# A planned order with the first scan step ranked ahead, and 360 filler products in place of 480

## The chip, the cores and the metric

The kernel runs on one core of one Trainium2 chip. The metric is device time in microseconds of one execution; before the change the median of three runs was 3912.99 us (3912.96 to 3919.06).

## What is computed

A block of four sublayers on an input of 8 batches x 512 tokens x 256 channels, in float32. Each sublayer is added to its input, which goes through a layer norm first:

```python
x = x + attention(layernorm(x), ...)
x = x + fp4_ffn(layernorm(x), w_gate, w_up, w_down)
x = x + mamba(layernorm(x), ...)
x = x + fp4_ffn(layernorm(x), w_gate, w_up, w_down)
```

- The attention has 16 heads of 16 channels, brought to 32 latent channels, with rotary positions, a causal mask and a softmax.
- The FFN has 704 hidden channels. Input, hidden and weights are quantised in blocks of 16 to a four-bit grid and scaled back; the gate goes through a SiLU.
- The mamba sublayer has a second norm and a residual of its own, a projection to 2 x 512 channels, and for each of two directions (forward, and backward in time) a causal convolution of 4 taps, a SiLU, and the recurrence `h = exp(dt*A)*h + dt*B*u`, `y = sum over 16 states of h*C`. The two results are merged by a product, gated and projected back.

## The kernel before

**The work of one batch.** All 512 tokens of a batch are handled together, channels on the 128 partitions and time along the row, or tokens on the partitions where a norm needs it. There are five kinds of work, each written as a Python generator that yields after every small piece:

- `attention`: projections into latents, `heads` for four groups of four heads (maxima of the scores by `L658`, `L660`, `L663`, `L668`; scores again, exponentials and products with the values by `L689`, `L691`, `L694`, `L699`), and the result x1 (`L584`, `L585`).
- `ffns`: `ffn_front` (norm by `L496`, quantising by `L723` to `L735`), `ffn_hidden` (`L802` to `L804`), `ffn_down` (`L818` to `L829`), in four blocks of 128 tokens. The first FFN reads x1 and stores x2; the second reads x4 and stores the output.
- `mamba_pre`: norm, projection, and eight convolutions (`L923` loads a diagonal filter, `L927` multiplies, `L928` to `L930` make the SiLU), whose results go to DRAM.
- `ssm_prep`: the products that give dt, B and C (`dbt` by `L1022`, dt by `L1038` to `L1052`), four times a batch.
- `ssm`, the scan, and `merge`, which makes x4.

**The scan** has 512 steps: 8 batches x 2 directions x 4 blocks of 128 channels x 8 pairs of states. One step multiplies `ub` by a row of B that is replicated over the partitions (`L1081`, DVE), computes two exponentials (`L1084`, ACT), scans twice (`L1086` forward or `L1088` backward, DVE), multiplies by a replicated row of C (`L1095`, POOL) and adds eight PE transposes into the PSUM tile `y` (`L1098`). The tile `h` has four buffers (`NHB`), `y` has one bank. Each step loads two replicas of 512 KB (`rep`).

**The order.** `interleave` runs the generators side by side: while batch b is scanned, batch b+3's attention, batch b+1's `mamba_pre`, batch b+2's first FFN and batch b-1's merge and second FFN are issued. For batch 0 there is a prologue without a scan: attention of batches 0 and 1, the first FFN and `mamba_pre` of batch 0. Then `issue_in_order` (L138) throws away the order of writing. It collects all instructions with their dependences and the buffer turns of each tile (`rings`), gives each a cost, and computes a rank from the end backwards: own cost plus the largest rank among those that need it or wait for its buffer. Then it plays the program through with these costs. An engine that is free takes, of what is ready, the instruction with the highest rank. The order that results is fixed by dependences, engine by engine. It is an order, not a timing: on the chip each engine works off its queue, and waits at its head by semaphores.

**The fillers.** In the prologue, `FILL` products of two constant tiles are written into a tile of the `y` bank (`L1189`). Nobody reads them. The order gives them rank -1, below everything, and each an earliest time in the planner's clock, 70000 ns plus 600 ns per filler: PE takes one whenever nothing else is ready. Since they hold the only `y` bank, the first transposes of the scan come after the last filler.

```python
idle = psum("y")
for _ in range(FILL):
    PE.matmul(idle.rearrange("p (a k) -> p a k", a=NT), idb, idb[:, None, :].to_broadcast([P, NT, P]), start=True, stop=True)
```

Of the kernel before, what the change touches and what calls it, by code (L numbers as in the profile page):

```python
# [59 lines left out]


DMA_LAT = 2300


def accesses(i):
# [72 lines left out]
def issue_in_order(tc, traced, rings, idle):  # L138
# [8 lines left out]
    hist, users, writers = {}, {}, {}  # L147
    for k, i in enumerate(ops):
        for name, lo, hi, p0, p1, _, psum, wr in acc[k]:
            h = hist.setdefault(name, [])  # L150
# [45 lines left out]
    port = [shared_port(i, a) for i, a in zip(ops, acc)]  # L196
    dma = [type(i).__name__ == "InstDMACopy" for i in ops]
    rank = [0.0] * n
    for k in reversed(range(n)):
        rank[k] = costs[k][1] * (1.2 if ops[k].engine == mybir.EngineType.DVE else 1.0) + DMA_LAT * dma[k] + max([rank[j] for j in succ[k] + behind[k]], default=0.0)  # L200
    at = [0.0] * n
    for c, k in enumerate(users[idle[0]]):
        rank[k], at[k] = -1.0, idle[1] + idle[2] * float(c)
# [9 lines left out]
    for _ in range(n):  # L213
        best = None
        for e, q in later.items():
            r, t = ready.setdefault(e, []), free.get(e, 0.0)
            while q and q[0][0] <= t:
                k = heapq.heappop(q)[1]
# [7 lines left out]
        while q and q[0][0] <= t:  # L226
            k = heapq.heappop(q)[1]
            heapq.heappush(r, (-rank[k], k))
        k = heapq.heappop(r)[1]
# [3 lines left out]
        if dma[k]:  # L233
            t = max(t, flying[0])
            m = ways(ops[k])
            lines[:m] = [max(t + 800, x) + costs[k][1] for x in lines[:m]]
            end = max(lines[:m]) + DMA_LAT - 800
            heapq.heapreplace(flying, end)
# [32 lines left out]
def tile_hybrid(ctx: ExitStack, tc: tile.TileContext, w: dict, consts: bass.AP, out: bass.AP):  # L271
# [18 lines left out]
    rings = {}  # L290
# [875 lines left out]
    def thread_s(b):  # L1166
        for d in range(2):
            nxt = None
            for k, _ in enumerate(ssm(b, d, scrs[b])):
                if k % 16 == PREP_AT:  # L1170
                    nxt = next(todo, None)
                    nxt = nxt and nxt()
                if nxt is not None and k % PREP_EV == 0:
                    next(nxt, None)
                yield
                if nxt is not None and k % 16 == 15:
                    for _ in nxt:
                        pass

    NA_, NB_, NS_ = 80, 100, 80  # L1180
    FILL, FILL_FROM, FILL_GAP = 480, 70000, 600
    PREP_AT, PREP_EV = 2, 2
    prep = {}
    af = {}
# [21 lines left out]
    first = thread_s(0)  # L1206
# [3 lines left out]
    for b in range(1, B):  # L1210
        run((NS_, OS, thread_s(b)), (NA_, OA, thread_a(b + 3)), (NB_, OB, thread_b(b - 1, b + 1, b + 2)))
    run((NB_, OB, thread_b(B - 1, B, B)))
    issue_in_order(tc, nc.cur_bb.bb.instructions, rings, (idle.name, FILL_FROM, FILL_GAP))


# [30 lines left out]
```

## Time and profile before

| | us |
|---|---|
| median of three runs | 3912.99 |
| the profiled execution | 3908.11 |
| its span (first to last instruction) | 3906.3 |
| PE busy | 3215.2 (82%) |
| DVE busy | 2953.2 (76%) |
| POOL busy | 2111.9 (54%) |
| ACT busy | 1740.7 (45%) |
| fillers (L1189): 480 records of 379 ns | first at 90.5, last at 641.5 |
| scan, first and last start on DVE (L1081) | 553.6 and 3772.0 |
| scan, first and last transposes on PE (L1098) | 642.0 and 3779.6 |

All times within the execution are counted from the first instruction. Records of PE products overlap, since the next one enters while the last one drains, so their sum is more than the time that PE is taken for. PEclk is the share of full clock that PE was granted. "Stretch" views give busy time of each engine between two moments; "by source line" views give, for one line of the kernel, its instructions with shortest, median and longest duration in ns and the first and last start in us.

### The profile page before, as it was taken

The page shows a single profiled execution, that of the slowest core. Times are in us where ns is not written, and L with a number is a line of the kernel's source. Part 1 is how long each engine was busy: PE and PEld are TensorE (multiplying, and loading weights), DVE is VectorE, ACT ScalarE, POOL GpSimd, SP SyncE. Part 2 cuts the span into 40 slices and gives each one's busy share as a digit, 9 for nine tenths or more (in the row PEclk, how much of TensorE's full clock was granted, in tenths as well). Part 3 has the DMA queues.
Part 4 walks back from the last instruction along what each step waited for, and adds up shares of the span by engine and source line. Part 5 has one row for each costly group of instructions (what it writes and reads, how often), then busy time and mean ns, then how long its engine had stood idle before and what let it go on. Part 6 is the DMA issues. An engine that isn't in the chain of part 4 may idle for free. (4 is left out here: it accounts for less than half of the span.)

```text
span 3906.3 us, 43657 instructions
## 1 busy us (share of the span) xinstructions
PE 3215.2 (82%) x13444; PEld 1843.7 (47%) x13444; DVE 2953.2 (76%) x3803; ACT 1740.7 (45%) x2989; POOL 2111.9 (54%) x1714
## 2 busy tenths in 40 slices
PE   5999999798889888798778888798878767767676
PEld 3444444444444545455444554445444544444553
DVE  5325256878988689886987779887888988888873
ACT  2222343555465344453455444554455445543421
POOL 4103134665675466654775546655576676666642
PEclk7999999899989988899889998799888978978888
DMA  6222354888777977689667896779767886995942
GB/s 167 82 80 69 121 192 131 269 282 271 232 263 257 304 241 238 212 274 294 218 222 231 258 297 204 245 254 315 236 218 261 290 314 215 326 352 174 366 151 71
DMA packets 439799, 898.19 MB, mean 230 GB/s; under 512 B 65005, under 2 KB 220046, under 8 KB 439566
## 3 DMA queue, kind: packets, MB, share of 16 engines
q1 hardware_dynamic: 439566, 895.40, 69.3%
q8 instruction: 108, 1.77, 0.2%
q14 instruction: 125, 1.02, 0.1%
HBM read 783.61 MB, written 103.15 MB: 227 GB/s over the span
## 5 line engine op out<-in xcount | busy, mean ns | idle before, releaser
L1095 POOL TENSOR_TENSOR h<-h,rep 128x1024 f32<-128x1024 f32 x512 | 1217.1, 2383 | 856.5 <-DVE h L1088 303.9
L1084 ACT ACTIVATE a<-dt,Aneg 128x512 f32<-128x512 f32 x1024 | 697.7, 689 | 561.4 <-DVE h L1088 265.1
L1098 PE MATMUL y<-cst,h 128*128 128x128 f32 x4096 | 693.5, 298 | 180.2 <-POOL h L1095 179.6
L1081 DVE TENSOR_TENSOR h<-ub,rep 128x1024 f32<-128x1024 f32 x512 | 616.6, 1210 | 206.7 <-PE y L1098 95.2
L1098 PEld LDWEIGHTS y<-cst,h 128*128 128x128 f32 x4096 | 529.7, 153 | 412.9 <-POOL h L1095 236.3
L1086 DVE TENSOR_TENSOR_SCAN h<-a,h 128x512 f32<-128x512 f32 x512 | 601.3, 1206 | 52.4 <-ACT a L1084 46.6
L1088 DVE TENSOR_TENSOR_SCAN h<-a,h 128x512 f32<-128x512 f32 x512 | 600.1, 1208 | 48.1 <-ACT a L1084 40.9
L314 PE MATMUL pb<-wgu,fxT 128*128 128x512 f32 (+1 forms) x768 | 372.9, 596 | 23.0 <-DVE hff L804 14.1
L699 PE MATMUL pa<-pt,vs 128*32 128x128 f32 (+3 forms) x1024 | 371.1, 458 | 13.0 <-ACT pt L694 10.3
L314 PE MATMUL pb<-qv,hff 128*128 128x256 f32 x1024 | 303.0, 422 | 85.3 <-DMA qv<-sy 74.6
L694 ACT ACTIVATE pt<-pa 128x512 f32<-128x512 f32 x320 | 190.3, 595 | 350.0 <-PE pa L691 347.8
L927 PE MATMUL pb<-xs,tmpB 128*128 128x512 f32 x512 | 272.6, 652 | 41.1 <-DMA tmpB<-dg_d 31.1
L658 PE MATMUL pa<-kst,qst 96*128 96x512 f32 (+3 forms) x512 | 211.2, 456 | 60.3 <-DVE mx L668 32.7
L314 PEld LDWEIGHTS pb<-qv,hff 128*128 128x128 f32 x1024 | 194.9, 209 | 137.9 <-issue 57.0
L314 PE MATMUL pb<-wdn,hT 128*128 128x256 f32 (+1 forms) x768 | 228.4, 420 | 18.1 <-ACT hT L821 7.1
L689 PE MATMUL pa<-qst,kst 98*128 98x512 f32 (+3 forms) x512 | 227.5, 449 | 14.3 <-ACT pt L694 12.2
L668 DVE TENSOR_REDUCE mx<-pa 128x1 f32<-128x512 f32 (+2 forms) x384 | 179.9, 501 | 61.4 <-PE pa L660 60.9
L314 PEld LDWEIGHTS pb<-wgu,fxT 128*128 128x128 f32 x768 | 134.3, 199 | 126.2 <-issue 85.5
L689 PEld LDWEIGHTS pa<-qst,kst 98*128 98x128 f32 x512 | 100.7, 197 | 180.8 <-issue 106.3
L314 PEld LDWEIGHTS pb<-wdn,hT 128*128 128x128 f32 (+1 forms) x768 | 142.5, 206 | 72.2 <-issue 28.4
L658 PEld LDWEIGHTS pa<-kst,qst 96*128 96x128 f32 x512 | 105.8, 209 | 133.7 <-DVE mx L668 43.1
L927 PEld LDWEIGHTS pb<-xs,tmpB 128*128 128x128 f32 x512 | 95.5, 208 | 132.7 <-issue 83.9
(217 smaller groups left out, 4882.3 us busy)
## 6 DMA issues: line engine op xcount, KB each, us to landing
rep<-bcd SPq DMA_DIRECT2D x1024, 512.0 KB
hld<-hl SPq DMA_DIRECT2D x64, 512.0 KB
hff<-in_merge_w SPq DMA_DIRECT2D x128, 256.0 KB
qv<-sy SPq DMA_DIRECT2D x128, 256.0 KB
kst<-hld SPq DMA_DIRECT2D x192, 128.0 KB
qst<-hld SPq DMA_DIRECT2D x192, 128.0 KB
tmpB<-dg_d SPq DMA_DIRECT2D x64, 256.0 KB
sxc<-tmpB SPq DMA_DIRECT2D x64, 256.0 KB
```

The source lines that it names most:

```text
L314: PE.matmul(o, L, R, start=start, stop=stop, **kw)
L658: PE.matmul(o[:, at : at + n], qst[pr][:96, j, i * P : (i + 1) * P], kst[:96, j, :n], start=(k == 0), stop=False)
L689: PE.matmul(o[:, at : at + n], kst[:, j, kt * P : (kt + 1) * P], qst[pr][:, j, kt * P :], start=(k == 0), stop=False)
L694: S.activation(pt, o, AF.Exp)
L699: PE.matmul(po[c : c + 32, kt * P :], vs[:, kt, h * VW : h * VW + 32], pt[:, at : at + n], start=(kt == 0), stop=(kt == 2), tile_position= ...
L927: PE.matmul(o, dg[:, k, :], xs[:, at : at + T], start=(k == 0), stop=(k == 3))
L1081: V.tensor_tensor(h, ub[:, None, :].to_broadcast([P, 2, T]), rb, ALU.mult)
L1084: S.activation(a, dt[:, m % 2, :], AF.Exp, scale=Aneg[:, d, m, 2 * n + e : 2 * n + e + 1])
L1086: V.tensor_tensor_scan(h[:, e], a, h[:, e], 0.0, ALU.mult, ALU.add)
L1088: V.tensor_tensor_scan(h[:, e, ::-1], a[:, ::-1], h[:, e, ::-1], 0.0, ALU.mult, ALU.add)
L1095: G.tensor_tensor(h, h, rc, ALU.mult)
L1098: PE.matmul(y[:, i * P : (i + 1) * P], h[:, e, i * P : (i + 1) * P], ident, start=(n == 0 and e == 0 and i == 0), stop=(n == NS // 2 - 1 a ...
```

## The change

The rank of one instruction, the first `L1081` of the scan, is raised by a million. Ranks are computed backwards, so every instruction that this step needs, directly or through others, or through a buffer that must come free, has a rank over a million too, and is taken before all that the first step does not need. Nothing after the first step changes its rank. The number of fillers goes from 480 to 360; their earliest times stay, 600 ns apart from 70000, so it is the last 120 that are gone. Four lines are added, and later lines stand 4 lower in the changed kernel (L1098 is L1102 there).

```diff
 DMA_LAT = 2300
+FIRST = 1e6
...
     rank = [0.0] * n
+    first = min(users[name][0] for name in rings["h"][1])
     for k in reversed(range(n)):
         rank[k] = costs[k][1] * (1.2 if ops[k].engine == mybir.EngineType.DVE else 1.0) + DMA_LAT * dma[k] + max([rank[j] for j in succ[k] + behind[k]], default=0.0)
+        if k == first:
+            rank[k] += FIRST
...
-    FILL, FILL_FROM, FILL_GAP = 480, 70000, 600
+    FILL, FILL_FROM, FILL_GAP = 360, 70000, 600
```

## The prediction

> **What bounds the kernel now.** I read the slices of the page first, to see where each engine is full.
>
> ```profile
> PE   5999999798889888798778888798878767767676
> ...
> DVE  5325256878988689886987779887888988888873
> ...
> PEclk7999999899989988899889998799888978978888
> ```
>
> A slice is 97.7 us. In slices 2 to 7 PE is full and DVE is at two to five tenths; from the seventh or eighth on DVE is near nine and PE near eight. So the kernel is two regimes: a PE-bound beginning without scan, and then the scan of 512 steps with DVE the fuller engine. Next I asked for busy times by stage (stretch, length, then busy us of PE, PEld, DVE, ACT, POOL, then clock, DMA share, GB/s):
>
> ```profile
> 289.00:406.00 117.00, 114.42 (x460) 52.48 (x458) 58.57 (x122) 32.29 (x69) 34.61 (x49) 1.00 0.22 70
> 406.00:553.00 147.00, 142.21 (x512) 60.96 (x512) 44.82 (x99) 61.70 (x107) 33.40 (x70) 0.99 0.47 148
> 553.00:642.00 89.00, 87.13 (x334) 38.34 (x332) 58.71 (x101) 32.07 (x62) 31.16 (x26) 1.00 0.41 128
> 642.00:1185.00 543.00, 458.14 (x1964) 254.08 (x1964) 464.10 (x580) 299.09 (x500) 343.15 (x271) 0.92 0.79 261
> 1200.00:2900.00 1700.00, 1432.71 (x6140) 835.63 (x6140) 1402.55 (x1753) 817.79 (x1389) 992.48 (x757) 0.91 0.76 249
> ```
>
> DVE works 58.57 of 117, 44.82 of 147 and 58.71 of 89 us, and then 85% in the fourth stretch. What separates the regimes is the line of the filler products, and the two lines of the scan beside it, in the answers by source line (L1189; then L1081 and L1098, both between 540 and 700 us):
>
> ```profile
> L1189 PE MATMUL y<-idb x480: 376/379/609, 90.5 to 641.5; 128*128 128x512 bf16 x160
> ```
>
> ```profile
> L1081 DVE TENSOR_TENSOR h<-ub,rep x14: 1186/1216/1225, 553.6 to 695.7; 128x1024 f32<-128x1024 f32 x14
> ```
>
> ```profile
> L1098 PE MATMUL y<-cst,h x89: 272/273/422, 642.0 to 699.8; 128*128 128x128 f32 x89
> ```
>
> The first scan step starts on DVE at 553.6. Its transposes into y start at 642.0, just after the last filler at 641.5: fillers own the only y bank. With four h buffers, four steps run and then the scan stands still until 646.8 (start of the fifth). That is a hole of 65 us in the scan, in a stretch where DVE has room.
>
> **What the change moves.** I compared the two built orders, fillers left out. They are the same up to the instruction that starts at 288 us on DVE and 294 us on PE, and the same again from 1166 (ACT) to 1208 us (SP) until the end: 2666 of 3805 DVE instructions and 7216 of PE's 10172 lie in the equal end. From about step 96 of the scan, then, the program is the old one, shifted. Only the shift is to be found. What lies after it, about 2700 us and the final merge and FFN, I cost at nothing, since it issues the same instructions in the same order.
>
> **Part 1, 120 fillers fewer.** Fillers follow each other in 0.216 us (starts of neighbouring records; the 379 ns of the row overlap). 120 x 0.216 = 25.9 us of PE time. Up to the split the old order has 332 fillers and the new one 337, so 148 are left in the old and 23 in the new. By itself that is worth between 0 and 26 us, as far as PE is the bound; it also frees the y bank early. The cover for fillers that stay is the wait of the attention chain before 289 us, where nothing changes.
>
> **Part 2, the first step earlier.** Its chain is attention of batch 0 (done in the equal part), FFN, mamba_pre, ssm_prep. Rows (L735 and L829 in the FFN of batch 0, and the same two lines in the last FFN, which runs alone):
>
> ```profile
> L735 POOL TENSOR_TENSOR fxn<-qv,qns x2: 1056/1056/1056, 306.7 to 310.8; 128x512 f32<-128x512 f32 x2
> ...
> L829 SPq DMA_DIRECT2D sx<-xrf x4: 342/343/425, 367.3 to 406.7; - x4
> ```
>
> ```profile
> L735 POOL TENSOR_TENSOR fxn<-qv,qns x2: 1056/1056/1056, 3854.7 to 3858.9; 128x512 f32<-128x512 f32 x2
> ...
> L829 SPq DMA_DIRECT2D out<-xrf x4: 332/338/338, 3886.2 to 3903.7; - x4
> ```
>
> From quantised input to last store: 406.7 - 310.8 = 95.9 us early, 3903.7 - 3858.9 = 44.8 us alone. In the new order a few attention products of batch 1 still stand between, so I take 51: stored at 362. Then 30.1 us to the first convolution, as before (406.7 to 436.8): 392.
>
> ```profile
> L927 PE MATMUL pb<-xs,tmpB x64: 591/593/697, 436.8 to 537.8; 128*128 128x512 f32 x64
> ```
>
> Eight convolutions start there at 436.8 to 521.1, 12.0 us apart. In the new order PE has 40 us of work between the first and the last start; the closest pairs anywhere in the trace stand 7.2 to 8.0 us apart. 7 x 8 = 56: last start at 448. Then 9.7 us to dbt (521.1 to 530.8) and 22.8 to the first h (530.8 to 553.6): **480 us instead of 553.6**. Bounds: 458 if all steps go as when alone, 508 if the FFN gains half as much and the convolutions stay 10 us apart. What the chain issues besides are loads on SP's queue: two replicas of 512 KB a step. The DMA share is 0.22 to 0.47 before 642, against 0.79 after, so there is room. POOL is 30% (34.61 of 117) and 23% busy there, room again.
>
> **Part 3, what is now behind.** Work that was ahead of the scan is behind it. I summed the orders with one cost for each form of instruction from this trace (DVE: median duration; PE: start to next start where PE is back to back, so 0.91 us for a 128x512 f32 product, 0.11 for a transpose, 0.216 for a filler). Ahead of the first y stand 554 us of PE work before, 365 after; ahead of step 24, 643 and 465; ahead of step 45, 740 and 672; ahead of step 96, 981 and 955. On DVE, ahead of the same steps: 227 and 175; 391 and 295; 497 and 476; 782 and 782. So 189 us of PE work leave the way of the scan, and 163 of them come back before step 96, most between steps 24 and 45. The sum is then made in three stretches, with DVE at the rate it held after the hole (step 4 to 96: 492 us of work in 646.8 to 1185.8, 0.913) and PE at 0.95, its rate between 289 and 642, and the larger of the two counts:
> - steps 0 to 24: DVE 121 / 0.913 = 132 us; PE 100 / 0.95 = 105. Takes 132.
> - steps 24 to 45: DVE 181 / 0.913 = 198; PE 207 / 0.95 = 218. PE ends last: 218.
> - steps 45 to 96: DVE 305 / 0.913 = 334; PE 283 / 0.95 = 298. Takes 334.
>
> 480 + 132 + 218 + 334 = 1164, where before step 96 started at 1185.8: **22 us earlier**. A gain of 74 us at the first step, and a hole of 65 us closed, shrinks since the two engines then have little slack left. The wait that takes the hole's place is DVE's and the scan's for PE in the second stretch. Bounds for this part: with DVE at 0.95 throughout, 127 + 218 + 321 = 666; with DVE at the 0.845 of the later batches (64 steps from 160 on: 367 us of DVE work in 436 us), 143 + 218 + 361 = 722. I take 0.913, as the nearest stretch with the same kind of work.
>
> The row that speaks against fewer fillers: where PE is kept full the granted clock is 1.00 (289 to 406), and in 642 to 1185, with PE 84% busy, 0.92. The new order leaves about 135 us of PE work in the 190 us before the first y, so the clock there should fall. [...]
>
> **Rivals.**
> A, DVE stays full all the way and the PE pile hides beside it: 607 us of DVE work / 0.95 = 639, 480 + 639 = 1119, 67 us earlier: **3846**. For it: 1135 to 1250 runs with both engines over nine tenths. Against: 207 us of PE work in 21 steps cannot go faster than 207.
> B, slower: the work of batches 1 and 2 that was put behind meets the scan between steps 24 and 45, and DVE and PE wait for each other as in the later batches (rate 0.845): 480 + 722 = 1202, 16 us later: **3929**. It decides from a stretch 24 to 45 over 240 us, or a DVE rate under 0.885 throughout. For it: new demand on both engines (PE 590, DVE 607 us of work) is nearer to the later batches' proportion than to that of 642 to 1185. Against: in the old order PE had to finish the same work, and did it while DVE idled.
> C, the change gives nothing: the first step's chain is not PE-bound but a chain of waits, the first h comes at 500 to 510, and the 22 us are gone: **3913**.
>
> **How the numbers follow.** The profiled execution took 3908.1 us (span 3906.3 and 1.8 around it); 3908.1 - 22 = 3886. The median of the three runs is 3913.0, 4.9 above that execution, so I forecast 3913 - 22 = **3891**. Chances: the forecast, 8 to 45 us gained, 0.48; A, more than that, 0.14; C, within 8 us (0.2%, about what a measurement of this kernel tells from no change), 0.15; B 0.23. So faster 0.62, same 0.15, slower 0.23. Range: from the best bounds (first h at 458, rate 0.95: 458 + 666 = 1124, 62 us gained) to B with a little to spare: 3850 to 3932.
>
> **What would show it.** First h at 480 (458 to 508), first y within 10 us of it, with no filler between; no pause of 65 us after the fourth step. Step 24 at about 612, step 45 at 830, step 96 at 1164, and all later steps earlier by the same amount. PE over 93% busy between steps 24 and 45. A first h after 510, or a step 45 after 850, would make the prediction wrong on the slow side; a step 45 before 800 on the fast side. If later steps are not shifted alike, the equal order did not carry the shift.

## The result

The changed kernel is slower, by 0.4%. Median of ten runs 3928.8 us (3920.93 to 3939.03) against 3912.97 us (3903.37 to 3921.88): ratio 1.0039, 95% interval 1.0027 to 1.0051. Forecast were 3891 us, in a range from 3850 to 3932, and faster with a chance of 0.62. The time lies in the range, the direction is wrong. It is the time of rival B (3929), though not for all of B's terms, as is shown further down.

The slices of the page after:

```profile
PE   5998888998979888798768888798887767767676
...
DVE  5324478668789779886987779887888988889873
...
PEclk7999989999989988899889998899888878978988
```

Slices are counted from 0 here (the prediction counts from 1). In 5 and 6 (491 to 687 us) DVE is at seven and eight tenths, where it was at five and six: the scan is early. But PE is at eight in slices 3 to 6 and no longer full, and in 7 and 8, where PE is at nine, DVE falls back to six. The same by stretches (length; busy us of PE, PEld, DVE, ACT, POOL; clock; DMA share; GB/s), first the changed kernel:

```profile
289.00:456.00 167.00, 148.15 (x475) 66.13 (x473) 57.21 (x113) 58.22 (x107) 43.55 (x66) 0.95 0.31 104
456.00:640.00 184.00, 146.21 (x622) 79.16 (x622) 148.33 (x187) 92.95 (x153) 108.19 (x84) 0.88 0.74 241
640.00:745.00 105.00, 102.02 (x419) 49.44 (x418) 64.95 (x110) 33.50 (x70) 32.83 (x27) 1.00 0.43 132
745.00:850.00 105.00, 93.79 (x377) 48.83 (x376) 70.91 (x109) 58.06 (x99) 55.30 (x61) 0.97 0.74 236
850.00:1200.00 350.00, 301.18 (x1253) 160.44 (x1252) 289.00 (x376) 181.12 (x310) 201.92 (x172) 0.92 0.73 236
1200.00:2900.00 1700.00, 1432.28 (x6140) 832.09 (x6139) 1400.37 (x1753) 808.58 (x1371) 989.72 (x759) 0.91 0.77 249
```

and the kernel before, cut at the same moments:

```profile
289.00:456.00 167.00, 163.02 (x657) 73.10 (x655) 75.20 (x164) 51.05 (x104) 45.67 (x88) 1.00 0.28 88
456.00:640.00 184.00, 178.79 (x641) 78.07 (x639) 86.89 (x157) 74.69 (x132) 53.50 (x57) 0.99 0.46 145
640.00:745.00 105.00, 87.49 (x412) 51.29 (x412) 80.20 (x104) 53.28 (x93) 57.08 (x44) 0.92 0.80 251
745.00:850.00 105.00, 85.33 (x373) 46.14 (x371) 86.76 (x105) 62.98 (x98) 69.48 (x47) 0.89 0.84 273
```

From 456 to 640 DVE does 148 us of work in place of 87, and PE 146 us in place of 179. From 640 to 850 it is the other way round: PE is 93% busy, and DVE has only 136 of 210 us, where it had 167. The last stretch, 1200 to 2900, is within 3 us of what it was (the row of the kernel before is in the prediction).

Now the lines that answer to those of before, by source line. Fillers, first scan product on DVE, transposes into y:

```profile
L1193 PE MATMUL y<-idb x360: 376/379/496, 89.6 to 302.5; 128*128 128x512 bf16 x180
```

```profile
L1085 DVE TENSOR_TENSOR h<-ub,rep x512: 1149/1211/1226, 456.3 to 3795.2; 128x1024 f32<-128x1024 f32 x171
```

```profile
L1102 PE MATMUL y<-cst,h x4096: 270/273/477, 462.7 to 3802.8; 128*128 128x128 f32 x196
```

The change did what it says: the last filler is at 302.5 in place of 641.5, the first step at 456.3 in place of 553.6, the first y 6.4 us behind it. What it gave up is in the line that ends a group of four heads (`L711`, L715 after), for batch 1, before and after:

```profile
L711 DVE TENSOR_TENSOR ya<-pa,rd x4: 425/425/425, 330.2 to 476.0; 128x256 f32<-128x256 f32 x4
```

```profile
L715 DVE TENSOR_TENSOR ya<-pa,rd x4: 424/424/425, 369.5 to 572.6; 128x256 f32<-128x256 f32 x4
```

The last group of batch 1 ends 97 us later. So the scan's first step comes 97 us earlier, and the end of that attention 97 us later. Along the scan, the lead of the changed kernel (starts of L1081 and L1085) is 97.3 us at step 0, 157.0 at step 24, 32.5 at step 45, 0.1 at step 70, and a lag of 15.8 at step 96. From there the lag stays between 11 and 19 us up to step 390; at the last step it is 23.2, and at the end 20.1 (spans of 3926.4 and 3906.3).

### The profile page after: what moved, and what is told of

Read it like the earlier page. It is cut to its first block, busy times and chain, and to the rows that moved or that the text cites. A ratio compares the mean times of both kernels' runs of the same rounds, so it can differ in the third digit from the quotient of the medians.

```text
span 3926.4 us, 43406 instructions
## 1 busy us (share of the span) xinstructions
PE 3202.5 (82%) x13324; PEld 1838.5 (47%) x13324; DVE 2964.7 (76%) x3803; ACT 1740.8 (44%) x2989; POOL 2114.5 (54%) x1714
## 5 line engine op out<-in xcount | busy, mean ns | idle before, releaser
L1102 PE MATMUL y<-cst,h 128*128 128x128 f32 x4096 | 693.2, 298 | 171.9 <-POOL h L1099 171.2
L1085 DVE TENSOR_TENSOR h<-ub,rep 128x1024 f32<-128x1024 f32 x512 | 616.1, 1208 | 199.0 <-PE y L1102 108.2
L1102 PEld LDWEIGHTS y<-cst,h 128*128 128x128 f32 x4096 | 528.2, 153 | 394.1 <-POOL h L1099 227.6
```

Source lines behind the costliest of these rows:

```text
L1085: V.tensor_tensor(h, ub[:, None, :].to_broadcast([P, 2, T]), rb, ALU.mult)
L1102: PE.matmul(y[:, i * P : (i + 1) * P], h[:, e, i * P : (i + 1) * P], ident, start=(n == 0 and e == 0 and i == 0), stop=(n == NS // 2 - 1 a ...
```

## The experiments

**Theory T**: the loss comes from the raised rank. The theory takes a million ns to be more than ranks differ by there, so that batch 1's attention falls behind batch 0's chain. From 456 to 640 us PE then has little but the scan's transposes and that attention to do. The attention is a chain of waits, and FFN and mamba_pre of batch 1, which would fill PE, cannot begin before it ends. They come as a pile from 640 to 850, and DVE waits. **Rival R1**: the loss comes from the missing fillers, by a lower clock. **Rival R2**: the loss comes from the early scan as such, which takes DVE and POOL from the other batches. Beside the times I use three quantities of each trace: the store of batch 1's x1 (the end of its attention), the start of step 96 on DVE, and PE's work without fillers from 456 to 640 us, with the costs per form of the prediction's part 3 (before 162 us, changed kernel 118 us, of which about 23 are the scan's transposes; before there are none of these). All ratios are to runs of the kernel before on the same chip. Its medians there were 3923.1 for the first four kernels, 3917.2 for the next four and 3914.4 for the last, so an expectation in us is read as its ratio to 3913.

**1. Fewer fillers alone** (`e1_fill360`, and once more as `e1b_fill360`)

```diff
# against the kernel before
-    FILL, FILL_FROM, FILL_GAP = 480, 70000, 600
+    FILL, FILL_FROM, FILL_GAP = 360, 70000, 600
```

> Only the fillers go from 480 to 360; the rank of the first scan step stays. Theory T (the loss comes from the raised rank, which pushes attention of batch 1 behind batch 0's chain, so that PE has only a chain of waits to work on from 456 to 640 us and a pile afterwards): batch 1's x1 is stored at 450 to 485 us, the first y comes at 530 to 560 us, time 3885 to 3905, faster than before. Rival R1 (the loss comes from fewer fillers, by a lower clock in the beginning): slower than before, 3920 to 3935. Rival R2 (the loss comes from the early scan itself, which takes DVE and POOL from attention and FFN of the next batches, whoever is ranked first): no faster than before, 3910 to 3930.

> 360 fillers, no rank raised, once more, on the chip of the others. Theory T: 0.994 to 0.999 of the kernel before, and up to 0.3% slower than with the first step and batch 1's attention raised, which starts the scan 15 to 20 us earlier.

Measured: 0.9966 (0.9945 to 0.9987) and 0.9969 (0.9949 to 0.9989), so faster. First y at 565.3 and 552.5 (T: 530 to 560), x1 of batch 1 at 499.5 and 489.6, later than the 485 that T allowed; PE's work from 456 to 640 is 147 and 142 us. R1 and R2 both wanted no gain. The half of the change that the prediction costed at 0 to 26 us is worth 12 or 13 (0.3%) by itself.

**2. The raised rank alone** (`e2_first480`)

```diff
# against the changed kernel
-    FILL, FILL_FROM, FILL_GAP = 360, 70000, 600
+    FILL, FILL_FROM, FILL_GAP = 480, 70000, 600
```

> Only the rank of the first scan step is raised; the fillers stay 480. Theory T: x1 of batch 1 is stored late as in the changed kernel (570 to 610 us), and the loss stays or grows by up to the 26 us that 120 fillers take: 3925 to 3955. R1: the clock is back and the loss with it: 3895 to 3915. R2: the fillers hold the y bank longer, so less early scan and less loss than in the changed kernel: 3910 to 3925.

Measured: 1.0019 (1.0002 to 1.0037), slower. The ratio is less than T's band (1.003 to 1.011), and fits R2's. R1 had the loss gone (at most 1.0005), which only the edge of the interval touches; with experiment 1 it is out. The trace has T's marks: x1 at 593.4, step 96 at 1200.7 (after: 1201.6), PE's work 115 us. It does not test R2, since the fillers ended early:

```profile
L1193 PE MATMUL y<-idb x480: 376/379/634, 90.4 to 481.1; 128*128 128x512 bf16 x160
```

With the rank raised, PE found time for all 480 by 481 us. Its interval overlaps with those of the changed kernel (1.0039 and 1.0045), so these runs can't tell 480 fillers from 360 once the rank is raised.

**3. Batch 1's attention raised as well** (`e3_attn1_too`, again as `e3b_attn1_too`)

```diff
# against the changed kernel
     first = min(users[name][0] for name in rings["h"][1])
+    ahead = {k for name in writers if name.startswith("sx1_1") for k in writers[name]}
...
-        if k == first:
+        if k == first or k in ahead:
             rank[k] += FIRST
```

> The changed kernel (360 fillers, first step raised), with the stores of x1 of batch 1 raised by the same amount, so that all attention of batch 1 is no longer behind the first step's chain. Theory T: x1 of batch 1 stored by 500 us, PE over 90% busy from 289 to 640 us, 3885 to 3905. R1: same fillers, so as slow as the changed kernel, 3920 to 3935. R2: the first y comes at 500 to 540, some 40 to 80 us later than in the changed kernel, so about half its loss: 3915 to 3925.

> The kernel with attention of batch 1 raised as well (360 fillers), once more. Theory T: 0.990 to 0.997 of the kernel before, step 96 at 1175 to 1190 us. R2 (early scan as such does the harm): 0.998 to 1.003. If the first reading was an accident of that chip, also 0.998 to 1.003.

Measured: 0.9932 (0.9910 to 0.9953) and 0.9944 (0.9922 to 0.9966). Step 96 at 1182.9 and 1171.1, x1 at 500.4 and 495.9, PE's work 147 and 149 us, first y at 554.6 and 546.6 (T had step 96 at 1175 to 1190; its "over 90% busy" holds from 289 to 456, with 93%, and is 89% after that). The stretches of the second:

```profile
289.00:456.00 167.00, 156.10 (x597) 70.88 (x595) 76.45 (x171) 51.90 (x106) 45.72 (x88) 0.97 0.28 89
456.00:640.00 184.00, 164.51 (x618) 79.08 (x619) 116.03 (x160) 88.68 (x147) 79.81 (x60) 0.93 0.68 221
640.00:745.00 105.00, 97.79 (x417) 49.85 (x416) 71.61 (x109) 50.56 (x93) 51.62 (x46) 0.95 0.51 164
745.00:850.00 105.00, 89.67 (x384) 46.02 (x383) 84.57 (x122) 56.87 (x96) 63.22 (x69) 0.97 0.76 253
```

From 456 to 850 PE is 85 to 93% busy and DVE 63 to 81%, where the changed kernel fell to 79% on PE and then to 62% on DVE. The scan begins 80 us later than in the changed kernel, and the kernel is 1% faster.

**4. The changed kernel again** (`a2_after`), on the chip of the second run of 3, of 5 and of the first run of 6.

> The changed kernel once more, to stand on the same chip as the next three. Both theories: 1.002 to 1.006 of the kernel before; step 96 of the scan at 1195 to 1208 us, x1 of batch 1 stored by about 599.

Measured: 1.0045 (1.0028 to 1.0061), 3934.75 us, beside 3890.92 for `e3b_attn1_too`. Step 96 at 1202.0, x1 at 596.8: these two marks repeat within 3 us.

**5. Half of the attention raised** (`e6_half_attn1`): two of batch 1's four groups of heads.

```diff
# against the kernel of experiment 3
-    ahead = {k for name in writers if name.startswith("sx1_1") for k in writers[name]}
+    ahead = {list(dict.fromkeys(writers[sorted(rings["ya"][1], key=lambda x: users[x][0])[1]]))[1]}
```

> The changed kernel with only the first two of batch 1's four groups of heads raised with the first step. Theory T, as a dose: x1 of batch 1 stored between the two ends, 535 to 565 us; PE's real work at 640 us behind the kernel before by 25 to 40 us (50 in the changed kernel, 19 with all four groups raised); time between them, 0.996 to 1.003 of the kernel before. R2: the first y comes at 480 to 520, so the scan competes nearly as early as in the changed kernel: 1.002 to 1.006.

Measured: 1.0026 (1.0010 to 1.0041), between 0.9944 and 1.0045 on that chip. x1 at 572.7, 8 us later than T's band; PE's work is 40 us behind the kernel before at 640 us. The dose counts, but R2's numbers fit as well (first y at 511.3), so this one does not decide.

**6. The scan held back** (`e7_hold`, then less long `e9_hold_less`): rank raised, fillers spread out so that they keep the y bank. The second has 1000 in place of 1150.

```diff
# against the changed kernel
-    FILL, FILL_FROM, FILL_GAP = 360, 70000, 600
+    FILL, FILL_FROM, FILL_GAP = 480, 70000, 1150
```

> The first step raised, but 480 fillers 1150 ns apart, so that they hold the y bank until about 600 to 650 us and the scan can't run on early. Theory T: batch 1's attention is still behind the chain until the first h (450 to 470 us), then has the engines to itself: x1 of batch 1 at 520 to 560, time 1.000 to 1.006 of the kernel before. R2: without the early scan no harm is left: 0.996 to 1.001, and PE's real work at 640 us level with the kernel before within 10 us.

> As the kernel that holds the y bank with 480 fillers 1150 ns apart, but 1000 ns apart, so that the hold ends about 60 to 150 us earlier than its 708 us. Theory T: batch 1's attention is behind the first step's chain as before, so x1 of batch 1 at 540 to 570 and still no better than the kernel before: 1.000 to 1.010. If most of the 1.015 came from the length of the hold, it falls with it; if the early scan were the harm, it would fall under 1.000.

Measured: 1.0152 (1.0132 to 1.0172), and 1.0048 (1.0025 to 1.0071). The last fillers:

```profile
L1193 PE MATMUL y<-idb x480: 377/379/634, 91.8 to 708.5; 128*128 128x512 bf16 x160
```

```profile
L1193 PE MATMUL y<-idb x480: 376/379/634, 88.2 to 559.3; 128*128 128x512 bf16 x160
```

The first hold was longer than meant (708.5, where the kernel before has 641.5), and its 1.0152 is outside both bands; part of it is that length. R2 had also said that PE's work up to 640 us would be level with the kernel before within 10 us; it is 44 us behind. The second hold ends at 559.3, 82 us before that of the kernel before, with the same 480 fillers; its first y (559.8) comes when that of experiment 1 does (565.3 and 552.5). It is slower than both, 1.0048 against 1 and against 0.9966 and 0.9969. x1 of batch 1 is at 564.8, step 96 at 1209.0. The scan is no earlier than in a faster kernel, and the harm is still there. Nor are fillers in the scan's way: none is left after 559.3, and from the fifth step, which starts at 563.2 here and at 564.7 in `e1b_fill360`, to step 96 this kernel takes 646 us and the other 610. What differs by then is batch 1: its second group of heads ended at 454.4 and not at 381.1, 5 us after the scan's first step (449.2) and with fewer fillers beside it than in the kernel before (87 and 103 from 289 to 456). So R2 is out as the cause of the loss. The stretches of `e9_hold_less`:

```profile
289.00:456.00 167.00, 158.34 (x541) 71.22 (x540) 63.73 (x118) 61.69 (x113) 43.76 (x57) 0.97 0.35 111
456.00:640.00 184.00, 166.38 (x729) 79.43 (x727) 94.99 (x150) 64.03 (x110) 63.67 (x67) 0.95 0.50 157
```

Here PE is 90% busy from 456 to 640, at a clock of 0.95. But 191 fillers are among it, 41 us; its other work is 110 us, still less than the changed kernel's 118. The scan does slow the attention, though: batch 1's third and fourth groups take 47 and 46 us here (ends at 454.4, 501.6 and 547.4), as in the kernel before (44 and 51), and 58 and 55 in the changed kernel, where the scan runs beside them. Held back or not, the time of the kernel is about the same (1.0048; 1.0039 and 1.0045).

**7. A smaller rank** (`e4_first1e5`)

```diff
# against the changed kernel
-FIRST = 1e6
+FIRST = 1e5
```

> The changed kernel with FIRST = 1e5 in place of 1e6: 100 us of rank, so that the chain of the first step goes ahead of what is less urgent by less than that; the order it gives keeps batch 1's attention where it was. Theory T: x1 of batch 1 by 505 us, 0.991 to 0.998 of the kernel before, as with attention raised too. If any raise of the first step did harm: over 1.001.

Measured: 0.9949 (0.9929 to 0.9969). x1 at 509.0 (T: by 505), first step at 540.6, step 96 at 1179.2, PE's work 147 us. So ranking the first step ahead does no harm by itself; the amount of 1000 us does.

**8. 240 fillers** (`e5_fill240` with the old rank, `e8_attn1_fill240` with that of experiment 3)

> The kernel before with 240 fillers, rank not raised. Theory T: 52 us less PE work than before; the first 120 removed gain 10 to 25 us, the next 120 were partly taken in waits that stay, so 0 to 15 us more: 3875 to 3905. R1: slower again than 360 fillers, over 3930. R2: about as 360 fillers or slower, 3910 to 3930.

> First step and batch 1's attention raised, 240 fillers in place of 360. Fillers take only PE time that nothing else wants as long as they end before the chain is full: 0.990 to 0.997 of the kernel before, the same as with 360 within 0.3%. If the clock mattered, slower than that by 0.3% or more.

Measured: 0.9974 (0.9953 to 0.9995), beside 0.9966 for 360 on that chip; 0.9960 (0.9938 to 0.9982), beside 0.9949 for experiment 7 on its chip. Another 120 fillers fewer change nothing that these runs can tell. The clock is no reason here. From 289 to 460 us it is 0.91 with 240 fillers, 1.00 with 480, and with 360 it is 0.92 in one profile and 1.00 in the other, of the same kernel (`e1_fill360`, `e1b_fill360`), while the two ratios are 0.9966 and 0.9969.

**What stands.** T holds by experiments 3, 6 and 7 above all: with batch 1's attention in its place the loss turns into a gain, and without an early scan it remains. The versions of experiments 3 and 7 beat both kernels (0.993 to 0.995). Whether the raised rank adds anything to fewer fillers is open: 0.9932 beside 0.9966 on one chip, 0.9949 and 0.9960 beside 0.9969 on another, all lower, but with intervals that overlap. Of the 184 us from 456 to 640, PE stood idle for 38 in the changed kernel (184 - 146.21) and for 5 before (184 - 178.79). What the lower clock there (0.88 and 0.99) cost by itself is open: in experiment 6 it was 0.95, but with the scan held, and no run raised it with the scan running.

## Why the prediction was wrong

**Part 1, fillers: right in place and size.** 0 to 26 us were set, 12 or 13 measured alone. The hole of 65 us in the scan closed, as said.

**Part 2, the first step: right in kind, and too cautious.** 456.3 against 480, 2 us outside the bounds (458 to 508). The terms of the sum: FFN stored at 350.7 where 362 stood, convolutions 6.5 us apart (380.4 to 425.8, seven intervals) where 8 stood. The lines of the stores and of the convolutions after:

```profile
L833 SPq DMA_DIRECT2D sx<-xrf x4: 319/320/343, 330.3 to 350.7; - x4
```

```profile
L931 PE MATMUL pb<-xs,tmpB x64: 590/592/697, 380.4 to 437.7; 128*128 128x512 f32 x64
```

The chain was held up by other work, not by its own waits, so rival C fell at once. The clock, which the prediction expected to fall ahead of the first y, was 0.95 from 289 to 456 us, where the kernel before had 1.00. The convolutions did not see the low part of it: 1.00 was granted from 372.8 to 444.5 us, while they ran, after 0.50 for the 14 us before (359.1 to 372.8).

**Part 3, the sum by stretches: this step failed.** The work in each stretch was right, since it comes from the orders. The rates were not. They were taken from times when both kinds of work were at hand, and PE's counts fillers: of PE's work from 289 to 640 us in the kernel before, 34 us are the 156 fillers there, and the rest is 298 us in 351, a rate of 0.85. At that rate the 207 us of the second stretch take 243.
- steps 0 to 24: 145 us in place of 132. DVE at 0.83 (121 / 145) and not 0.913.
- steps 24 to 45: 247 in place of 218. PE at 0.84 (207 / 247) and not 0.95. The pile did come, PE was 93% busy from 640 to 850, but the stretch began at 602, and until 640 PE was still in the thin part (23 us of work in 38). Over the whole stretch it was 91% busy, where over 93% was said.
- steps 45 to 96: 353 in place of 334. DVE at 0.865 (305 / 353). The prediction's own sign of being slow, step 45 after 850, did not show (848.9); these 19 us come after it. No run separates why this stretch is slow as well.

Together 745 us in place of 684, 61 too many; 24 fewer in the first step; so 38 us between the forecast and the measured step 96 (1164 and 1201.6), and the sign with it. Rival B had named the place (work put behind meets the scan between steps 24 and 45) and the mark to know it by: a stretch over 240 us, or DVE under 0.885 throughout. Measured were 247 us and 607 / 745 = 0.81. That its time was met to the microsecond is in part luck: its first step came 24 us earlier than its 480, and its 218 for steps 24 to 45 was 29 too few. It had engines waiting for each other, and no chain. It was given 0.23 because "in the old order PE had to finish the same work, and did it while DVE idled". That reason was the mistake. In the old order, two independent chains lay beside each other in the beginning, FFN and mamba_pre of batch 0 and attention of batch 1, and fillers took the rest. Serving one first and the other afterwards leaves PE with one chain at a time. That cost little up to 456 us (130 us of work in place of 136), and much after it. The profile before showed what one chain alone does to PE. In batch 0's attention (100 to 289 us) PE was full only because fillers took what the attention left (301 of them, 65 of 189 us). Its groups of heads there:

```profile
L711 DVE TENSOR_TENSOR ya<-pa,rd x4: 424/424/425, 129.9 to 264.3; 128x256 f32<-128x256 f32 x4
```

134.4 / 3 = 44.8 us for a group with nothing but fillers beside it; no group in the kernel before took less than 44. In the changed kernel batch 1's second group took 90 us behind the chain (369.5 to 460.0), and the third and fourth 58 and 55 beside the scan. Of the 97 us of delay, 79 were there at the second group (460.0 and 381.1 before), when the scan had just begun. So what is late after the first step is not an engine that is full but a chain of about 45 us a group at best, and a queue of work behind its end. I summed engine work in the order of the queues, and that sum does not see a chain. PE's own waits from 456 to 640 us show the chain at work (who waited, for whom: us in total, times, longest), in the changed kernel:

```profile
PE pa L662 <- DVE mx L672: 7.3, 8, 1.3
PE pa L693 <- ACT pt L698: 4.3, 4, 2.9
PE pa L348 <- ACT tmp L708: 3.1, 2, 1.6
PE pa L662 <- DVE tmp L618: 3.1, 2, 2.6
```

and in the kernel before, its three longest:

```profile
PE pa L689 <- ACT pt L694: 2.2, 1, 2.2
PE pa L344 <- DVE mx L663: 1.1, 2, 0.8
PE pa L658 <- DVE hl L635: 0.6, 2, 0.3
```

PE waits for the maxima, which DVE makes beside the scan, and for the exponentials of ACT: the three engines hand one group of heads to and fro. ACT's wait for the scores is no sign of it, since it was longer before (38.1 us, and 27.1 in the changed kernel).

The changed kernel draws the scan 97 us further into the beginning, where PE leads (before, from 456 to 640 us, PE had 179 us of work and DVE 87; after, DVE has 148). Here it did not pay, 1.0039, since two chains that both feed PE were put in sequence for it: PE's work without fillers fell from 136 + 162 us (289 to 456, 456 to 640) to 130 + 118.

**The equal order** did carry the shift: 15.8 us at step 96, 17.9 at step 390. The 4 us more at the end (20.1) come from equal instructions, and lie within what the profiles of equal ends differ by (below).

## What to carry to other kernels

A list scheduler's rank says which ready work goes first; a bonus larger than the differences between ranks makes an order of precedence out of it, and takes the second chain away that kept the other engines fed. Raise by a bounded amount, and look at what falls behind: here, both with 360 fillers, 100 us of rank ended at 0.9949 of the kernel before and 1000 us at 1.004. A gap in the most visible work (the scan's 65 us hole) is worth little when the engine that must feed the next stages was full during it. A rate measured while fillers ran counts the fillers, and is no rate for real work (0.95 with them, 0.85 without). In a sum over engine queues, ask for every stretch whether there are two independent chains at hand; if only one is left, use the time of the chain (here 45 us a group), not the rate of an engine.

## What the runs showed of the hardware

The granted clock of one stretch can differ between two executions of one kernel. With 360 fillers and the old rank, twice, first `e1_fill360`, then `e1b_fill360`:

```profile
407.50:434.80 27.30, 25.27 (x63) 9.30 (x63) 1.86 (x9) 9.57 (x18) 4.09 (x20) 0.50 0.33 95
```

```profile
407.50:434.80 27.30, 24.03 (x102) 11.35 (x102) 7.70 (x27) 12.17 (x23) 4.16 (x21) 1.00 0.46 128
```

PE is 93 and 88% busy there, and gets through 63 records at 0.50 and 102 at 1.00. The first y comes at 565.3 and 552.5. So a clock of one profile is not a property of the order.

From step 96 to the start of the last step the same instructions in the same order took 2586.1 us (before), 2593.6 and 2599.3 (the changed kernel twice) and 2602.7 to 2607.1 (experiment 3, twice) in single profiled executions. The two profiled executions of experiment 3 were the slowest of their runs (3923.7 and 3909.8 us, medians 3894.6 and 3890.9). So 10 us of difference between two profiles' ends need no cause in the order, and times within 0.2% are not to be told apart by single executions.
